# Counting the conv slices and the transfers double, and fetching one step-size tile earlier, in a two-layer kernel (convolutional layer and selective scan)

## The chip, the core and the metric

The kernel runs on one core of one Trainium2 chip. The metric is the device time of one execution in microseconds (us). The core's engines are TensorE (PE, matrix multiply; its weight loads are shown as PEld), VectorE (DVE), ScalarE (ACT), GpSimd (POOL) and SyncE (SP). In this kernel SP issues every DMA. Each engine takes its own instructions strictly in order and waits, where it must, on semaphores.

## What is computed

The input x is 16 images of 64 x 64 pixels with 96 channels in float32. Two layers follow one another, each with a group normalisation in front and a residual sum behind:

```
x = x + L0(gn(x))   # upsample 64->100 by a spectral filter, h = W1 u, h = c0 + c1 h + c2 h^2, W2 h, downsample
x = x + L1(gn(x))   # xz = x Win; xc = silu(conv3x3(xc)); z = silu(z)
                    # 4 directions: delta = softplus(...); h_t = exp(delta_t A) h_(t-1) + delta_t u_t B_t; y_t = C_t h_t
                    # sum of directions, layer norm, times z, times Wout
```

The scan is the large part: 4 directions x 192 channels x 16 states, each over 4096 pixels.

## The kernel before, in words

**The scan, in units.** `scan()` cuts one image into 8 steps (4 pieces of 1024 pixels, first for directions pair 0, then in the opposite order for pair 1), a step into 6 blocks of channels, a block into 4 quarters j = 0 to 3 of the states. One such piece is a *unit* n: 192 units to an image, 3072 in all. A unit has two halves e = 1 and e = 0, each 128 partitions x 1024. Its work is

- ACT: `decay`, da = exp(delta a), once for each half (L788), into PSUM;
- POOL: `drive`, b = dtu * bt for both halves at once (L794), issued two units ahead;
- DVE: `recur`, the scan itself (L803 or L805), once for each half, and the product with ct for half 0 (L972);
- the product with ct for half 1: on POOL (L963), or, in every fifth unit by a running credit (`SHARE`), on DVE (L954). Such a unit is called *odd* below;
- `keep` (L811): the last column goes to the next step's start, for half 1 by DVE (by ACT in an odd unit);
- PE: `read_out` of the unit before (L827), 16 matmuls that sum the states into y.

The order within a unit is written out by hand (L947 to L994): recur(n,1), its product, decay(n+1,1), **slot 0**; POOL's product, drive(n+2); recur(n,0), read_out(n-1), **slot 1**; DVE's product for half 0, decay(n+1,0), **slot 2**; then DMA issues for what comes later.

**What runs in the slots.** Three generators give the other work, a slice at a time (a slice is what stands between two `yield`s):

- `project` makes delta, delta*u and the rows B and C for the next step (PE, ACT, one DVE product at L702, DMAs to DRAM); it has its own pace (`PSLICES`);
- `front(mi+1)`, the first layer of the next image, its norms, and at the end the 3x3 convolution of the second layer with silu: 12 tiles (L482 to L510), 4 with 64 rows (i = 1), 8 with 128 rows (i = 0);
- `finish(mi-1)`, the end of the second layer of the image before; it starts when `front` has ended.

**The pace.** `Background` counts slots in `at` and slices in `n`. A slice is due while n * positions < at * slices. For front and finish positions is 576 (192 units x 3 slots) and slices is `SLICES` = 499. A slice that yields nothing counts 1 and one that yields HEAVY counts 2. A slice that yields WAIT counts 1 too: it ends ahead of the two silu of a convolution tile, and the next slice then runs only in a slot 2 in which it is due (the *gate*, L887); the unit after a gate is made odd (`full_unit`). The credit goes negative by that and no other unit is odd until it is made up, so the number of odd units stays 614.

A silu needs another table in ACT than exp does. A gate therefore puts on ACT: a table load, silu of c_ps (L506), silu of z_ps (L507), a table load back (L508). The two PSUM banks that front and finish share (`b_ps`, bufs=2) hold c_ps and z_ps until then.

**The transfers and tiles that the change touches.** `parts` (L196) moves one image of 96 or 128 rows in 4 (or 2) DMAs, one to a slice: the load of x (L250), the store of x1 (L453), the store of the transposed convolution (L514), the loads of ycol in finish (L529, L530). `fetch_delta` (L726) loads the step sizes of one half of a block (128 x 1024, 512 KB). The pool has three buffers. For the next block, half 1 is fetched in the unit with j = 1, half 0 in the unit with j = 2, behind slot 2 (L980); half 0's buffer is the one that decay(n+1,1) of this same unit reads last.

In `norm` (called twice in front) DVE multiplies two columns of 96 x 1, nb = nmean * rg (L237); behind the first norm it adds 96 x 96, lin = lin + ident (L260).

Of the kernel before, what the change touches and what calls it, by code (L numbers as in the profile page):

```python
# [68 lines left out]
NEPS = 1e-5  # L69
BOTH = "natural_log_exp_and_others"  # L70
POS = 3 * 8 * 6 * NQ
SLICES = 499
WAIT = -1
BUSY = -2
HEAVY = 2
# [5 lines left out]
def tile_two_blocks(  # L81
# [114 lines left out]
    def parts(out, in_, n=4):  # L196

        step = L // n
        for i in range(n):
            nc.sync.dma_start(out=out[:, step * i:step * i + step], in_=in_[:, step * i:step * i + step])  # L200
            yield

    def norm(xt):

# [36 lines left out]
    def front(mi):  # L241
# [225 lines left out]
        for i, n, tiles, both in ((1, 64, 4, 4), (0, 128, 8, 0)):  # L467
            col = b16.tile([128, tiles * TB], F32, name="col", tag="b16")
            halves = [(n * k, t0) for k, t0 in enumerate((0, both)[:128 // n])]
            turned = None  # L470

            def turn(t, row, z):
                nc.scalar.copy(
                    col.rearrange("c (w h) -> c w h", w=HW)[:, :, 8 * t:8 * t + 8],
                    row.rearrange("c (h w) -> c w h", w=HW),
                )
                for p, t0 in halves:
                    cols = slice(TB * (t + t0), TB * (t + t0) + TB)
                    nc.sync.dma_start(out=made["xs"][2 * i, 0:n, cols], in_=row[p:p + n])
                    nc.sync.dma_start(out=made["z"][128 * i:128 * i + n, cols], in_=z[p:p + n])  # L480

            for t in range(tiles):  # L482
                c_ps = bank([128, 8, HW], "c_ps")
                for tap in range(9):
                    dy, dx = divmod(tap, 3)
                    for p, t0 in halves:
                        h0 = 8 * (t + t0) + dy
                        nc.tensor.matmul(  # L488
                            c_ps[p:p + n], lhsT=wtap_s[:, tap, 128 * i:128 * i + n],
                            rhs=xgp[:, h0:h0 + 8, dx:dx + HW], start=(tap == 0), stop=(tap == 8),  # L490
                            skip_group_check=True,
                        )
                    if tap == 3 and turned is not None:
                        turn(*turned)
                    if tap % 2 == 1:
                        yield
                z_ps = bank([128, 8, HW], "z_ps")
                for p, t0 in halves:
                    h0 = 8 * (t + t0) + 1
                    nc.tensor.matmul(  # L500
                        z_ps[p:p + n], lhsT=zwt_s[:, 128 * i:128 * i + n], rhs=xgp[:, h0:h0 + 8, 1:HW + 1],
                        start=True, stop=True, skip_group_check=True,
                    )
                yield WAIT
                row, z = piece([128, TB], "row"), piece([128, TB], "z")
                nc.scalar.activation(row, c_ps.rearrange("c h w -> c (h w)"), AF.Silu, bias=convb_s[:, i:i + 1])  # L506
                nc.scalar.activation(z, z_ps.rearrange("c h w -> c (h w)"), AF.Silu)  # L507
                nc.scalar.preload_act_table_set(BOTH)  # L508
                turned = t, row, z
                yield  # L510
            turn(*turned)
            yield HEAVY
            if i == 0:
                yield from parts(made["xs"][1], col)  # L514
            else:
                for p, t0 in halves:
                    to = made["xs"][2, 64:128, :].rearrange("c (w h) -> c w h", h=HW)
                    for w0 in range(0, HW, 16):
                        nc.sync.dma_start(
                            out=to[:, w0:w0 + 16, 8 * t0:8 * t0 + 32],  # L520
                            in_=col[p:p + n].rearrange("c (w h) -> c w h", w=HW)[:, w0:w0 + 16, :],
                        )
                        yield HEAVY
# [99 lines left out]
    def scan():  # L623


        with ExitStack() as es:
# [99 lines left out]
            def fetch_delta(ctx, bi, e):  # L726
                t = p3.tile([128, T], F32, name="delta")
                spread(t, "delta", ctx, bi, e)
                return t
# [21 lines left out]
            bc, dtus, deltas = {}, {}, {}  # L751
# [103 lines left out]
            class Background:  # L855
# [11 lines left out]
                def step(self):  # L867
                    self.said = next(self.gen, 0)
                    if self.said == 0:
                        self.gen = None  # L870
                    else:
                        self.n += self.said if self.said is not None and self.said > 0 else 1

                def drain(self):
                    while self.gen is not None:
# [40 lines left out]
            for n, (st, bi, j) in enumerate(units):  # L916
                mi, pair, lc = steps[st]
                v, s0, r = blocks[bi]
                m = n // NQ
                if n % per_image == 0:  # L920
                    image[mi]["y"] = dram.tile([2, DI, L], F32, name="y_d")
                    behind_gen.drain()
                    ahead_gen = behind_gen = nothing
                    if mi + 1 < B:
                        ahead_gen = Background(front(mi + 1), SLICES, POS)
                elif n % per_image == 2 and mi > 0:
                    behind_gen = Background(finish(mi - 1), SLICES, POS)
                if j == 0:
                    new = stp.tile([128, 2, NQ], F32, name="new", tag=f"st{bi}")
                    states[bi] = (states[bi][1] if states[bi] else None, new)  # L930

                if j == 0:
                    ahead = None
                    if bi + 1 < len(blocks):
                        ahead = ctxs[st], bi + 1
                    elif n + NQ <= last:
                        step_gen.drain()
                        ahead = ctxs[st + 1], 0
                        next_step(st + 2, mi)
                    if ahead:  # L940
                        dtus[m + 1] = fetch_dtu(*ahead)
                elif j == 1:
                    if ahead:
                        deltas[m + 1, 1] = fetch_delta(*ahead, 1)


                credit += 1  # L947
                odd_here = n == full_unit or credit >= SHARE
                if odd_here:
                    credit -= SHARE  # L950
                h = das[n, 1] if odd_here else bs[n][:, 1, :]
                recur(n, 1, h)
                if odd_here:
                    nc.vector.tensor_mul(bs[n][:, 1, :], h, bc[1, r, j])  # L954
                keep(n, 1, h, nc.scalar.copy if odd_here else nc.vector.tensor_copy)
                if n < last:
                    decay(n + 1, 1)
                slot(0)
                if storing is not None:
                    next(storing, 0)  # L960
                    storing = None
                if not odd_here:
                    nc.gpsimd.tensor_mul(h, h, bc[1, r, j])  # L963
                if n + 2 <= last:
                    drive(n + 2)

                h = das[n, 0]
                recur(n, 0, h)
                if n >= 1:
                    read_out(n - 1)  # L970
                slot(1)
                nc.vector.tensor_mul(bs[n][:, 0, :], h, bc[1, r, j])  # L972
                keep(n, 0, h, nc.scalar.copy)
                if n < last:
                    decay(n + 1, 0)
                if n >= 1 and units[n - 1][2] == NQ - 1:
                    storing = store(n - 1)
                    next(storing)
                slot(2)
                if j == 2 and ahead:  # L980
                    deltas[m + 1, 0] = fetch_delta(*ahead, 0)
                if j == NQ - 1 and n < last and steps[units[n + 1][0]][1] == 1:
                    st2, bi2, _ = units[n + 1]
                    y0s[steps[st2][2], bi2] = fetch_y0(steps[st2][2], bi2)


                at = n % per_step
                for what in range(2):
                    ahead_j = at - (2 * NQ - 1 + what)
                    if 0 <= ahead_j < NQ:  # L990
                        bc[what, 1, ahead_j] = fetch_bc(ctxs[st], 1, ahead_j, what)
                    ahead_j = at - (5 * NQ - 1 + what)
                    if 0 <= ahead_j < NQ and st + 1 < len(steps):
                        bc[what, 0, ahead_j] = fetch_bc(ctxs[st + 1], 0, ahead_j, what)  # L994
# [113 lines left out]
```

## Time and profile before

| what | value |
|---|---|
| median of 3 runs | 21079.41 us (21074.11 to 21098.74) |
| the profiled execution's own time | 21085.42 us |
| its span, first to last instruction | 21083.6 us |
| granted TensorE clock, mean | 0.860 |
| DMA queue of SP, share of 16 engines | 60.1% |

The page gives busy time by engine over the whole span, then groups of instructions. A group's line has its count, its total busy time, the mean of one in ns, and behind the bar the idle time of its engine just before it with what ended most of it. A line of a timeline has the start in us, the duration, engine, line, operation, and in brackets the idle time before it with its releaser.

### The profile page before, as it was taken

The page shows a single profiled execution, that of the slowest core. Times are in us where ns is not written, and L with a number is a line of the kernel's source. Part 1 is how long each engine was busy: PE and PEld are TensorE (multiplying, and loading weights), DVE is VectorE, ACT ScalarE, POOL GpSimd, SP SyncE. Part 2 cuts the span into 40 slices and gives each one's busy share as a digit, 9 for nine tenths or more (in the row PEclk, how much of TensorE's full clock was granted, in tenths as well). Part 3 has the DMA queues.
Part 4 walks back from the last instruction along what each step waited for, and adds up shares of the span by engine and source line. Part 5 has one row for each costly group of instructions (what it writes and reads, how often), then busy time and mean ns, then how long its engine had stood idle before and what let it go on. Part 6 is the DMA issues. An engine that isn't in the chain of part 4 may idle for free. (4 is left out here: it accounts for less than half of the span.)

```text
span 21083.6 us, 273452 instructions
## 1 busy us (share of the span) xinstructions
PE 16908.7 (80%) x98988; PEld 7230.6 (34%) x98988; DVE 19569.4 (93%) x12983; ACT 13780.9 (65%) x20546; POOL 19498.8 (92%) x5538
## 2 busy tenths in 40 slices
PE   7876788888878788788788888888787787888856
PEld 4423324233343333324333242333433333243221
DVE  0999999999999999999999999999999999999997
ACT  4666666667666666666666666676666666666553
POOL 0999999999999999999999999999999999999996
PEclk8887888888889888898888988888898888988977
DMA  2565565655656566565665656556565665656654
GB/s 84 191 202 195 195 227 195 221 202 196 226 198 227 197 210 212 194 230 191 218 207 197 226 199 219 202 197 222 197 226 198 212 212 198 229 195 216 224 186 141
DMA packets 1855464, 4277.11 MB, mean 203 GB/s; under 512 B 449438, under 2 KB 548670, under 8 KB 1852062
## 3 DMA queue, kind: packets, MB, share of 16 engines
q1 hardware_dynamic: 1854110, 4259.62, 60.1%
q8 instruction: 781, 12.80, 0.3%
q14 instruction: 573, 4.69, 0.1%
HBM read 3380.58 MB, written 878.18 MB: 202 GB/s over the span
## 5 line engine op out<-in xcount | busy, mean ns | idle before, releaser
L794 POOL TENSOR_TENSOR b<-dtu,bt 128x2048 f32<-128x2048 f32 x3072 | 13895.8, 4532 | 581.2 <-DMA dtu<-dtu_d 465.1
L788 ACT ACTIVATE da<-delta,a_s 128x1024 f32<-128x1024 f32 x6144 | 6857.4, 1117 | 2562.1 <-DVE b L972 945.5
L963 POOL TENSOR_TENSOR b<-b,ct 128x1024 f32<-128x1024 f32 x2458 | 5797.1, 2358 | 836.9 <-DVE new L811 628.6
L827 PE MATMUL y<-b,fold_s 128*32 128x256 f32 x49152 | 3871.3, 437 | 1153.0 <-DVE b L972 680.8
L972 DVE TENSOR_TENSOR b<-da,ct 128x1024 f32<-128x1024 f32 x3072 | 3756.4, 1223 | 91.8
L803 DVE TENSOR_TENSOR_SCAN da<-da,new,b 128x1024 f32<-128x1024 f32 x1383 | 3245.3, 2347 | 72.7 <-ACT da L788 57.2
L805 DVE TENSOR_TENSOR_SCAN da<-da,new,b 128x1024 f32<-128x1024 f32 x1361 | 3193.0, 2346 | 99.7 <-ACT da L788 77.0
L827 PEld LDWEIGHTS y<-b,fold_s 128*32 128x32 f32 x49152 | 1388.5, 119 | 3876.9 <-issue 1464.0
L805 DVE TENSOR_TENSOR_SCAN b<-da,new,b 128x1024 f32<-128x1024 f32 x943 | 2208.7, 2342 | 139.3 <-ACT da L788 81.5
L803 DVE TENSOR_TENSOR_SCAN b<-da,new,b 128x1024 f32<-128x1024 f32 x921 | 2156.5, 2341 | 11.2 <-ACT da L788 10.5
L811 ACT COPY new<-da 128x1 f32<-128x1 f32 x2764 | 432.9, 157 | 2607.4 <-DVE b L972 2236.0
L488 PE MATMUL c_ps<-xgp,wtap_s 96*64 96x512 f32 (+1 forms) x4608 | 1728.2, 633 | 184.7 <-ACT row L506 179.4
L697 PE MATMUL s<-w,ident_s 128*128 128x512 f32 x1530 | 1167.2, 854 | 636.0 <-ACT w L692 614.2
L371 PE MATMUL h_ps<-xu,w1t_s 96*128 96x500 f32 x1920 | 1044.0, 643 | 299.9 <-ACT t L311 125.9
L383 PE MATMUL o_ps<-w2c_s,hsq 128*100 128x96 f32 x9600 | 1041.5, 266 | 178.1 <-ACT hsq L352 177.8
L677 PE MATMUL s<-pr,dtw_s 128*128 128x512 f32 x1530 | 928.5, 691 | 315.2 <-ACT delta L703 224.9
L805 DVE TENSOR_TENSOR_SCAN da<-da,b 128x1024 f32<-128x1024 f32 x482 | 1103.5, 2289 | 53.0 <-ACT da L788 43.1
L383 PEld LDWEIGHTS o_ps<-w2c_s,hsq 128*100 128x100 f32 x9600 | 975.0, 179 | 410.3 <-ACT hsq L352 232.1
L803 DVE TENSOR_TENSOR_SCAN da<-da,b 128x1024 f32<-128x1024 f32 x460 | 1053.0, 2289 | 36.8 <-ACT da L788 34.8
L697 PE MATMUL s<-e,ident_s 128*128 128x512 f32 x1530 | 1004.2, 745 | 0.0
L820 PE MATMUL y<-y,ident_s 128*128 128x512 f32 x768 | 524.2, 770 | 583.5 <-ACT yt L838 457.6
L488 PEld LDWEIGHTS c_ps<-xgp,wtap_s 96*64 96x64 f32 (+1 forms) x4608 | 583.1, 169 | 1121.7 <-issue 842.6
(143 smaller groups left out, 21936.5 us busy)
## 6 DMA issues: line engine op xcount, KB each, us to landing
dtu<-dtu_d SPq DMA_DIRECT2D x1536, 512.0 KB
delta<-delta_d SPq DMA_DIRECT2D x1536, 512.0 KB
bt<-rows SPq DMA_DIRECT2D x1024, 512.0 KB
ct<-rows SPq DMA_DIRECT2D x1024, 512.0 KB
u<-xs_d SPq DMA_DIRECT2D x893, 256.0 KB
dtu_d<-dtu SPq DMA_DIRECT2D x765, 256.0 KB
delta_d<-delta SPq DMA_DIRECT2D x765, 256.0 KB
xr<-in_x SPq DMA_DIRECT2D x768, 128.0 KB
```

The lines of the kernel that those rows point to most:

```text
L371: nc.tensor.matmul(h_ps[j], lhsT=w1t_s[:, 128 * j:128 * (j + 1)], rhs=xu.rearrange("c p q -> c (p q)"), start=True, stop=True,)
L383: nc.tensor.matmul(o_ps[:, p, :], lhsT=hsq[j][:, UPS * p:UPS * (p + 1)], rhs=w2c_s[:, j, :], start=(j == 0), stop=(j == HB - 1),)
L488: nc.tensor.matmul(c_ps[p:p + n], lhsT=wtap_s[:, tap, 128 * i:128 * i + n], rhs=xgp[:, h0:h0 + 8, dx:dx + HW], start=(tap == 0), stop=(tap ...
L677: nc.tensor.matmul(s, lhsT=dtw_s[:, pair, v, :], rhs=pr, start=True, stop=True)
L697: nc.tensor.matmul(s, lhsT=ident_s, rhs=of, start=(k == 0), stop=(k == 3))
L788: nc.scalar.activation(da, deltas[n // NQ, e], AF.Exp, scale=a_s[:, k, g, units[n][2]:units[n][2] + 1])
L794: nc.gpsimd.tensor_mul(b, dtus[n // NQ], bt.unsqueeze(1).to_broadcast([128, 2, T]))
L803: nc.vector.tensor_tensor_scan(out, da, b, before, ALU.mult, ALU.add)
L805: nc.vector.tensor_tensor_scan(out[:, ::-1], da[:, ::-1], b[:, ::-1], before, ALU.mult, ALU.add)
L827: nc.tensor.matmul(y[32 * q:32 * q + 32, e, :], lhsT=fold_s, rhs=b[:, e, QT * q:QT * q + QT], start=(pair == 0 and j == 0 and e == 0), sto ...
L963: nc.gpsimd.tensor_mul(h, h, bc[1, r, j])
L972: nc.vector.tensor_mul(bs[n][:, 0, :], h, bc[1, r, j])
```

## The change

```
-SLICES = 499
+SLICES = 541
...
     def parts(out, in_, n=4):
...
             nc.sync.dma_start(out=out[:, step * i:step * i + step], in_=in_[:, step * i:step * i + step])
-            yield
+            yield HEAVY
...
                 nc.scalar.activation(z, z_ps.rearrange("c h w -> c (h w)"), AF.Silu)
                 nc.scalar.preload_act_table_set(BOTH)
                 turned = t, row, z
-                yield
+                yield HEAVY
...
                 def step(self):
...
-                        self.n += self.said if self.said is not None and self.said > 0 else 1
+                        self.n += self.said if self.said is not None and self.said > 0 else HEAVY if self.said == WAIT else 1
...
                 slot(0)
+                if j == 2 and ahead:
+                    deltas[m + 1, 0] = fetch_delta(*ahead, 0)
...
                 slot(2)
-                if j == 2 and ahead:
-                    deltas[m + 1, 0] = fetch_delta(*ahead, 0)
```

No instruction is added or taken away. Every slice of `parts`, and two of the six slices of each convolution tile (the one that ends in WAIT and the one with the silu), count 2 instead of 1; the pace of front and finish is 541 counts to 576 slots instead of 499; and the fetch of delta for half 0 is issued behind slot 0 of its unit instead of behind slot 2.

More of the change, by code (lines that the diff above doesn't have):

```diff
@@ L71 @@
 POS = 3 * 8 * 6 * NQ
-SLICES = 499
+SLICES = 541
 WAIT = -1
@@ L200, in parts @@
             nc.sync.dma_start(out=out[:, step * i:step * i + step], in_=in_[:, step * i:step * i + step])
-            yield
+            yield HEAVY
     def norm(xt):
@@ L509, in front @@
                 turned = t, row, z
-                yield
+                yield HEAVY
             turn(*turned)
@@ L871, in step @@
                     else:
-                        self.n += self.said if self.said is not None and self.said > 0 else 1
+                        self.n += self.said if self.said is not None and self.said > 0 else HEAVY if self.said == WAIT else 1
                 def drain(self):
@@ L958, in scan @@
                 slot(0)
+                if j == 2 and ahead:
+                    deltas[m + 1, 0] = fetch_delta(*ahead, 0)
                 if storing is not None:
@@ L979, in scan @@
                 slot(2)
-                if j == 2 and ahead:
-                    deltas[m + 1, 0] = fetch_delta(*ahead, 0)
                 if j == NQ - 1 and n < last and steps[units[n + 1][0]][1] == 1:
```

## The prediction

> **What bounds the kernel now.** I read the page first: two engines are nearly full, and no chain shows one culprit (its largest share is 1%).
>
> ```profile
> ## 1 busy us (share of the span) xinstructions
> PE 16908.7 (80%) x98988; PEld 7230.6 (34%) x98988; DVE 19569.4 (93%) x12983; ACT 13780.9 (65%) x20546; POOL 19498.8 (92%) x5538
> ```
>
> Then POOL's groups. POOL does nothing but two products, and their number is fixed, so its time is a floor; what can be gained is its idle time.
>
> ```profile
> L794 POOL TENSOR_TENSOR b<-dtu,bt 128x2048 f32<-128x2048 f32 x3072 | 13895.8, 4532 | 581.2 <-DMA dtu<-dtu_d 465.1
> L963 POOL TENSOR_TENSOR b<-b,ct 128x1024 f32<-128x1024 f32 x2458 | 5797.1, 2358 | 836.9 <-DVE new L811 628.6
> ```
>
> The 465.1 us are the start-up (image 0's front, alone). The rest I placed from the trace's rows: idle ahead of each POOL product, by unit, and the time from one image's first scan to the next. The 15 images that have a front behind them take 1279.7 us on average (1272.6 to 1287.7); the last, without one, 1225. A unit's POOL work is 4.53 + 0.8 x 2.36 = 6.42 us, so 192 units are 1232 us, and POOL idles 60.6 us an image (908.8 / 15). Of these, about 31.5 us fall in units 106 to 146, the convolution (units 104 to 140); 8.5 us in units 5 to 19 (first norm), 8.3 us in units 99 to 105 (second norm), 8.0 us in units 20 to 98, 4.0 us behind. The last image has 16.6 us in all. So: **two engines in balance, POOL a little ahead as the floor, and half of the loss in a fifth of the image.**
>
> The stretch of the convolution, by windows of image 5 (columns: us; then busy us and count of PE, PEld, DVE, ACT, POOL; clock; DMA share; GB/s): four tiles, a transfer, eight tiles, a transfer, and the five units of the second line below.
>
> ```profile
> 7700.00:7835.00 135.00, 125.05 (x541) 48.93 (x539) 124.27 (x83) 102.57 (x141) 117.14 (x33) 0.96 0.55 187
> 7741.00:7779.00 38.00, 37.99 (x167) 15.44 (x166) 32.62 (x22) 29.99 (x42) 27.75 (x9) 0.98 0.67 224
> ```
>
> In the second line PE is busy for all of 38 us and POOL for 27.75: here neither DVE nor POOL but PE is late. The timeline of the gate inside it:
>
> ```profile
> 7749.52 1.28 ACT L506 ACT_TABLE_LOAD   x1
> 7753.63 0.69 ACT L506 ACTIVATE row<-c_ps,convb_s 128x512 f32<-128x512 f32 x1 [2.83 <-PE c_ps L488]
> 7754.49 0.60 ACT L507 ACTIVATE z<-z_ps 128x512 f32<-128x512 f32 x1 [0.17 <-PE z_ps L500]
> 7755.10 1.28 ACT L508 ACT_TABLE_LOAD   x1
> ...
> 7757.81 2.35 DVE L805 TENSOR_TENSOR_SCAN b<-da,new,b 128x1024 f32<-128x1024 f32 x1 [2.09 <-ACT da L788]
> ...
> 7760.49 2.35 POOL L963 TENSOR_TENSOR b<-b,ct 128x1024 f32<-128x1024 f32 x1 [3.31 <-DVE new L811]
> ```
>
> ACT loads the table, waits 2.83 us for c_ps, and the exp behind it comes late; DVE waits 2.09 us for that exp, POOL 3.31 us for DVE. A gate's own ACT work is 1.28 + 0.69 + 0.60 + 1.28 = 3.85 us.
>
> **The change, part by part.**
>
> *Pace and conv counts (SLICES 541, WAIT and silu slices 2).* Front counted 368 and ends at 368 x 576 / 499 = slot 425 (unit 141). Now it counts 368 + 12 (parts) + 24 (12 tiles x 2) = 404 and ends at 404 x 576 / 541 = slot 430 (unit 143). A tile takes 6 x 576 / 499 = 6.93 slots = 2.31 units now and 8 x 576 / 541 = 8.52 slots = 2.84 units then; all else of front comes 541/499 = 8.4% denser, and the convolution starts at unit 99 instead of 104. Counting slices through gives the gates. Before: 106, 109, 111, 113; 122, 125, 127, 129, 131, 134, 137, 139. After: 101, 105, 107, 110; 119, 122, 125, 127, 130, 133, 137, 139. So gates two units behind another fall from six (111, 113, 127, 129, 131, 139) to three (107, 127, 139).
>
> POOL's idle between a gate and the next, mean of images 1 to 14: for those six 6.10, 2.99, 6.33, 3.26, 4.14, 1.96, mean 4.13 us. For the other six (106, 109, 122, 125, 134, 137) 0.82, 0.88, 0.34, 1.83, 1.32, 1.48, mean 1.11 us. Sum 31.45. After: 3 x 4.13 + 9 x 1.11 = 22.4; giving gates at distance three or four their own mean (1.38) and the first of a run 0.58, 23.2. I take 23.2: **8.2 us an image less.** Ends: if the three cost like the cheapest pair (1.96 and 2.99, mean 2.5), 17.5 and 14 less; like the dearest (6.2), 28.4 and 3 less. The reason that the mean should hold: ACT's waits for c_ps (L506) come only at 111 (1.14), 127 (3.90), 129 (1.53) and 131 (1.74 us), all two behind another and with a single slot from the z_ps matmul to the silu. Afterwards only three tiles have a single slot, the others three to seven. PE's load in the eight tiles falls too: 125 of 135 us before; 8 x 0.53 = 4.2 more units bring 27 us of time (6.4 each), of which the stalls gone take 8, but only some 11 us of PE work (a unit: 1.07 for the 16 matmuls of L827, an estimated 1.6 for project): 136 of 154, 88%. When the stall goes, DVE is late next: an odd unit costs it about 1.1 us more, and gates at three make one unit in three odd. That part stays.
>
> *Denser front, units 8 to 95.* Nothing new is issued; the same work lies 8.4% closer. ACT is 67% busy there (379 of 562 us), PE 82% (462.8). POOL's 8.0 us of idle in units 20 to 98 grow by 8% if they go with density, 0.7; I take +1 us; ends 0 and +5.
>
> *First norm.* nb (L237) moves from unit 6 slot 2 to unit 7 slot 2, lin (L260) from unit 7 slot 2 to unit 8 slot 1. These DVE products of two SBUF tiles stand still while POOL runs:
>
> ```profile
> 7557.02 4.49 POOL L794 TENSOR_TENSOR b<-dtu,bt 128x2048 f32<-128x2048 f32 x1
> 7561.48 2.35 POOL L963 TENSOR_TENSOR b<-b,ct 128x1024 f32<-128x1024 f32 x1
> 7563.80 4.48 POOL L794 TENSOR_TENSOR b<-dtu,bt 128x2048 f32<-128x2048 f32 x1
> 7574.53 2.35 POOL L963 TENSOR_TENSOR b<-b,ct 128x1024 f32<-128x1024 f32 x1 [6.25 <-DVE new L811]
> ```
>
> nb began at 7560.16 and took 8.14 us, to 7568.30: to the end of the last of three POOL products. Behind slot 2 one scan (2.35) stands between the release and POOL's next L963; behind slot 1, a product more (1.22). So lin costs +1.2, taken as **+1 us an image**; ends -1 and +5 (the worst images of the second norm idle 13.2 where the mean is 8.3). The second norm's nb moves from unit 101 slot 0 to unit 96 slot 0, five units, the odd units' own period: 0. The Trainium skill, SBUF — State Buffer, "SBUF: two separate sides", says that a VectorE operation with two SBUF inputs and a GpSimd operation exclude each other and that the loser waits for the one that started first to end; by that rule nb would cost at most one product. The row differs: it lasted over two starts of POOL, and up to 12.3 us in other images, so here the wait ends when POOL pauses. By the rule the ends of this term would be -1 and +1.
>
> *Delta earlier and parts spread.* ACT's waits for delta are 123.9 us in 56 times, at two units of an image above all (144 and 148, 4 to 5 us each), behind the burst of four 512 KB stores and six loads of ycol.
>
> ```profile
> ACT da L788 <- DMA delta<-delta_d: 123.9, 56, 5.3
> ```
>
> Both parts of the change shorten that, but POOL idles only 1.4 us in units 144 to 151, where no unit is odd and POOL's 6.88 us a unit hide DVE. So -1 us; ends -2 and 0. What is moved: the fetch waits on SP for decay(n+1,1), issued on ACT just ahead of slot 0; behind it on SP now stand what slots 1 and 2 issue (project's and front's DMAs). Those were made by instructions later on ACT and DVE anyway; only loads (xr, u) lose a few us of a lead of several slots: 0. finish starts at slot 430 and ends at unit 190 as before: 0.
>
> Sum: -8.2 + 1 + 1 - 1 = -7.2 us an image, x 15 = **-108 us**; 21085.4 - 108 = 20977. The median shown is 6 us below the profiled execution, so 20970.
>
> **The rivals.**
> 1. *Spacing is not what costs* (same). If each of the 12 gates costs its 2.6 us (31.45 / 12) wherever it stands, conv gives 0 and the rest +1 an image: 21,094; anything from 21,040 to 21,100. For it: gate 139 stands two behind another and cost 1.96, gate 125 three behind and 1.83. Against: 6.1 and 6.3 at 111 and 127.
> 2. *PE gets colder* (slower). The clock was 0.96 to 1.00 in the crowded conv windows and 0.85 in the front stretch (units 8 to 95); c_ps matmuls took from 590 to 1222 ns. If spreading lets the clock fall to 0.85, PE's 88% becomes 101% (0.98 x 0.88 / 0.85) and the eight gates of the 128-row tiles cost 4.13 each, the other four 1.11: 37.5 us, +6.0 an image, with +1 from the rest +105 us: 21,185. It decides from a clock of about 0.91 down, where PE's load passes 95%. Against: PE's gaps there are short.
> 3. *All gates get cheap* (faster). At 1.1 to 1.4 us each: 13 to 17 us, 14 to 18 less an image: 20,830 to 20,870.
>
> **How the numbers follow.** Forecast 0.62 (20,880 to 21,035), rival 1 0.17, rival 2 0.12, rival 3 0.09. A measurement tells some 0.2% (42 us) from no change, so faster is below 21,037: 0.62 + 0.09 = 0.71; same 0.17; slower 0.12. The range runs from 20,860 to 21,100, which leaves out rival 2 and half of rival 3.
>
> **What would show it.** POOL's idle before L963 by DVE new falls from 628.6 to some 500 us; ACT's wait for c_ps (170.3 us, 72 times) falls below 100; ACT's wait for delta falls below 60 us; PE is no longer full in any window of 38 us; the clock there stays above 0.93. Wrong if POOL's idle in the conv stretch stays at 31 us an image, if nb and lin take longer than 10 us on average, or if the gain sits in units 8 to 95.

## The result, and the profile after

The changed kernel takes 21084.27 us (median of 12 runs) against 21084.57 us for the kernel before (12 runs); the ratio is 0.9999, 95% interval 0.9991 to 1.0007. That is no difference that can be told. Predicted were 20970 us and a gain of 0.5%.

The page of the changed kernel: span and busy times, then POOL's two groups (L965 is the product that stood in L963).

```profile
span 21080.5 us, 273502 instructions
## 1 busy us (share of the span) xinstructions
PE 16801.4 (80%) x98988; PEld 7116.5 (34%) x98988; DVE 19514.0 (93%) x12983; ACT 13777.9 (65%) x20546; POOL 19499.7 (93%) x5538
...
L794 POOL TENSOR_TENSOR b<-dtu,bt 128x2048 f32<-128x2048 f32 x3072 | 13902.2, 4534 | 522.6 <-DMA dtu<-dtu_d 465.0
...
L965 POOL TENSOR_TENSOR b<-b,ct 128x1024 f32<-128x1024 f32 x2458 | 5805.7, 2362 | 892.1 <-DVE new L811 453.4
```

POOL's work is the same, and so is its idle time: 581.2 + 836.9 before, 522.6 + 892.1 after. The waits of POOL in the changed kernel show where a reader can be misled:

```profile
POOL b L965 <- DVE new L811: 453.4, 249, 16.7
POOL b L965 <- issue: 310.2, 79, 13.8
```

The wait for DVE's `new` fell as forecast (628.6 to 453.4), but the part put down to "issue" rose from 131.1 to 310.2 us. Both come from a late DVE: in 78 of the 79 waits put down to "issue" a `new` of DVE had ended less than 0.3 us before the product began. So only their sum counts, and it stayed: 760 and 764 us.

Placed by unit as in the prediction (us of POOL idle an image, mean of images 1 to 14; the second norm stands in units 99 to 105 before and 94 to 100 after):

| stretch | before | predicted | after |
|---|---|---|---|
| units 0 to 19 (first norm) | 8.5 | 9.5 | 4.9 |
| up to the second norm | 8.0 | 9.0 | 7.2 |
| second norm | 8.3 | 8.3 | 8.5 |
| convolution, to unit 146 | 31.5 | 23.3 | **34.9** |
| rest | 4.0 | 3.0 | 3.6 |
| sum | 60.4 | 53.2 | 59.1 |

14 images gain 1.3 us each, image 0 loses 14.9 us (63.6 to 78.5), the last is even: -3.3 us, and the spans differ by -3.1. So the question is why the convolution did not get cheaper. Its windows in image 5 (the conv from unit 120 on; the five units around gate 127):

```profile
7700.00:7850.00 150.00, 128.95 (x550) 50.50 (x550) 136.26 (x90) 111.95 (x154) 130.00 (x37) 0.91 0.54 181
7751.50:7789.00 37.50, 33.67 (x155) 13.27 (x154) 33.21 (x22) 28.45 (x40) 30.39 (x9) 0.96 0.75 251
```

PE did come down, from 38.0 of 38 us to 33.7 of 37.5, and POOL is fuller there. That step held. The loss went elsewhere, to gates that were cheap before. POOL's idle behind each gate:

| before: gate | 106 | 109 | 111 | 113 | 122 | 125 | 127 | 129 | 131 | 134 | 137 | 139 |
|---|---|---|---|---|---|---|---|---|---|---|---|---|
| us | 0.8 | 0.9 | 6.1 | 3.0 | 0.3 | 1.8 | 6.3 | 3.3 | 4.1 | 1.3 | 1.5 | 2.0 |
| **after: gate** | 101 | 105 | 107 | 110 | 119 | 122 | 125 | 127 | 130 | 133 | 137 | 139 |
| us | 6.6 | 0.6 | 5.5 | 1.3 | 0.0 | 3.6 | 1.8 | 5.2 | 3.3 | 3.8 | 1.5 | 1.7 |

The timeline of gate 101 in the changed kernel, image 5:

```profile
7576.90 0.60 ACT L685 ACTIVATE e<-s 128x512 f32<-128x512 f32 x1 [3.00 <-PE s L677]
7577.53 0.63 ACT L686 ACTIVATE e<-e 128x512 f32<-128x512 f32 x1
...
7579.38 1.28 ACT L506 ACT_TABLE_LOAD   x1
...
7581.87 1.28 ACT L508 ACT_TABLE_LOAD   x1
...
7584.57 2.29 DVE L805 TENSOR_TENSOR_SCAN b<-da,b 128x1024 f32<-128x1024 f32 x1 [1.62 <-ACT da L788]
...
7587.19 2.37 POOL L965 TENSOR_TENSOR b<-b,ct 128x1024 f32<-128x1024 f32 x1 [3.37 <-issue]
...
7588.35 0.71 ACT L692 ACTIVATE w<-w,one_s 128x512 f32<-128x512 f32 x1
...
7589.51 1.12 PE L697 MATMUL s<-w,ident_s 128*128 128x512 f32 x2
...
7593.25 0.69 DVE L702 TENSOR_TENSOR dtu<-s,u 128x512 f32<-128x512 f32 x1 [1.86 <-PE s L697]
...
7596.47 2.36 POOL L965 TENSOR_TENSOR b<-b,ct 128x1024 f32<-128x1024 f32 x1 [2.43 <-DVE new L811]
```

`project` works on ACT in a chain: abs and exp (L685, L686), relu and w (L688, L689), ln and w (L691, L692); then come four matmuls on PE (L697) and one product on DVE (L702). Here the chain has begun when the gate opens. ACT first waits 3.00 us for project's matmul, which stands on PE behind convolution taps, then runs the gate's 3.85 us, and only then the rest of the chain; a first stall of DVE (1.62) follows. The chain's last step ends twelve us after its first began. PE, at the next taps until then, starts the four matmuls of L697 0.45 us after that, and DVE, which has its product L702 in order between two scans, stands for 1.86 us. POOL idles twice, 3.37 and 2.43 us. Below, a gate is called *straddled* when its silu are issued between e and ln of one chain. In the kernel before three of twelve are straddled (109, 122, 125), in the changed one five (101, 122, 125, 130, 133).

### The profile page after: what moved, and what is told of

Read it like the earlier page. It is cut to its first block, busy times and chain, and to the rows that moved or that the text cites. A ratio compares the mean times of both kernels' runs of the same rounds, so it can differ in the third digit from the quotient of the medians.

```text
span 21080.5 us, 273502 instructions
## 1 busy us (share of the span) xinstructions
PE 16801.4 (80%) x98988; PEld 7116.5 (34%) x98988; DVE 19514.0 (93%) x12983; ACT 13777.9 (65%) x20546; POOL 19499.7 (93%) x5538
## 3 DMA queue, kind: packets, MB, share of 16 engines
q1 hardware_dynamic: 1854110, 4259.62, 60.6%
## 5 line engine op out<-in xcount | busy, mean ns | idle before, releaser
L794 POOL TENSOR_TENSOR b<-dtu,bt 128x2048 f32<-128x2048 f32 x3072 | 13902.2, 4534 | 522.6 <-DMA dtu<-dtu_d 465.0
L965 POOL TENSOR_TENSOR b<-b,ct 128x1024 f32<-128x1024 f32 x2458 | 5805.7, 2362 | 892.1 <-DVE new L811 453.4
L488 PE MATMUL c_ps<-xgp,wtap_s 96*64 96x512 f32 (+1 forms) x4608 | 1784.0, 652 | 299.1 <-ACT row L506 293.7
L697 PE MATMUL s<-w,ident_s 128*128 128x512 f32 x1530 | 1185.5, 867 | 685.4 <-ACT w L692 640.3
L383 PE MATMUL o_ps<-w2c_s,hsq 128*100 128x96 f32 x9600 | 993.7, 260 | 99.1 <-ACT hsq L352 66.4
L697 PE MATMUL s<-e,ident_s 128*128 128x512 f32 x1530 | 1032.6, 765 | 0.0
L383 PEld LDWEIGHTS o_ps<-w2c_s,hsq 128*100 128x100 f32 x9600 | 928.3, 172 | 298.2 <-issue 128.1
```

The costliest lines, as they stand in the source:

```text
L383: nc.tensor.matmul(o_ps[:, p, :], lhsT=hsq[j][:, UPS * p:UPS * (p + 1)], rhs=w2c_s[:, j, :], start=(j == 0), stop=(j == HB - 1),)
L488: nc.tensor.matmul(c_ps[p:p + n], lhsT=wtap_s[:, tap, 128 * i:128 * i + n], rhs=xgp[:, h0:h0 + 8, dx:dx + HW], start=(tap == 0), stop=(tap ...
L697: nc.tensor.matmul(s, lhsT=ident_s, rhs=of, start=(k == 0), stop=(k == 3))
L794: nc.gpsimd.tensor_mul(b, dtus[n // NQ], bt.unsqueeze(1).to_broadcast([128, 2, T]))
```

## The experiments

Theory A (the spacing theory of the expectations) is that of the prediction: a gate two units behind another is dear. Theory B (the alignment theory): a gate is dear where it straddles project's chain or where PE is late, and the change only moved the gates to other places of the chain. "After" is the changed kernel. A ratio is to the kernel before as measured beside the run; differences to after are between medians taken at different times, over which the kernel before moved from 21084.6 to 21095.3 us.

**One part at a time, e1 to e3.** e1 is the kernel before with the delta fetch moved alone:

```
                 slot(0)
+                if j == 2 and ahead:
+                    deltas[m + 1, 0] = fetch_delta(*ahead, 0)
...
                 slot(2)
-                if j == 2 and ahead:
-                    deltas[m + 1, 0] = fetch_delta(*ahead, 0)
```

> The kernel before with one part of the change: delta of half 0 is fetched behind slot 0 instead of behind slot 2. The gates stand as before. Spacing theory (mine, as predicted: a gate two units behind another costs 4.1 us of POOL idle, another 1.1) and alignment theory (a gate is dear where the softplus chain of project, from its first exp to w, straddles it or where PE is late with c_ps, wherever the gates stand) both say: POOL idle between units 106 and 146 stays at 31.5 us an image, time within 0.1% (0 to -25 us). If the early fetch holds up SP, slower by more than 40 us.

Measured: ratio to before 0.9998 (0.9989 to 1.0007), 31.9 us in the convolution. ACT's waits for delta fell from 123.9 to 75.1 us, and nobody gained by it.

e2 counts the slices of `parts` double:

```
-SLICES = 499
+SLICES = 515
...
-            yield
+            yield HEAVY
```

> The kernel before with the slices of parts counted double, and 515 slices so that front ends in the same slot (380 x 576 / 515 = 425). Gates 106, 109, 111, 113, 121, 125, 127, 129, 131, 133, 135, 137: eight of twelve stand two behind another; two are straddled by the chain. Spacing theory: conv idle 8 x 4.1 + 4 x 1.1 = 37 us an image, 80 us slower than before. Alignment theory: about as before (two straddled instead of three, more tiles of one slot), 28 to 34 us, same time within 40 us.

Measured: 1.0000 (0.9991 to 1.0009); 32.1 us in the convolution, though eight gates stand two behind another; A said 37. Waits for delta: 76.4 us. With both parts, in the changed kernel, they are 1.2 us, still without effect on the time.

e3 counts double the slice behind the silu and, in `step`, the one that ends in WAIT:

```
-SLICES = 499
+SLICES = 531
...
-                yield
+                yield HEAVY
...
-                        self.n += self.said if self.said is not None and self.said > 0 else 1
+                        self.n += self.said if self.said is not None and self.said > 0 else HEAVY if self.said == WAIT else 1
```

> The kernel before with two slices of each conv tile counted double, and 531 slices so that front ends in the same slot (392 x 576 / 531 = 425). Gates 101, 103, 106, 109, 118, 121, 125, 127, 130, 133, 135, 138: three of twelve two behind another (103, 127, 135), but five straddled by the chain (101, 106, 109, 125, 130, 133 counting the one whose chain had just begun: six). Spacing theory: conv idle 22 to 23 us an image, some 125 us faster than before. Alignment theory: 35 us or more, no faster than before.

Measured: **1.0148 (1.0134 to 1.0162), slower by 313 us**; 44.2 us in the convolution. The straddled gates 106, 109, 130, 133 cost 6.3, 6.3, 5.2, 2.9; the straddled 101 and 125 only 0.8 and 0.9. The rest of the loss lies behind the convolution (10.8 instead of 4.0 us) and ahead of it (12.2 instead of 8.0). A falls as the whole story: it had said 125 us faster.

**The gates moved by a unit or two, e4.**

```
+        for _ in range(2):
+            yield
         for i, n, tiles, both in ((1, 64, 4, 4), (0, 128, 8, 0)):
```

> The changed kernel with two empty slices ahead of the convolution, so that the gates move by one or two units: 102, 105, 107, 110, 119, 122, 125, 129, 131, 134, 137, 139. As in the changed kernel three stand two behind another; but only two (122, 125) are straddled by the chain of project, where five are in the changed kernel (101, 122, 125, 130, 133). Spacing theory: as the changed kernel, within 25 us. Alignment theory: three straddled gates fewer at some 3 us each, 9 us an image, 100 to 150 us faster than the changed kernel.

Measured: 21017 us, ratio to before 0.9964 (0.9951 to 0.9976), 67 us faster than after. The convolution fell from 34.9 to 26.2 us, in sum as B said (9 us). Gate by gate it is less clear: 102, 129 and 134 cost 1.2, 0.9 and 1.5 (101, 127 and 133 had cost 6.6, 5.2 and 3.8), but 125, straddled as before, rose from 1.8 to 5.8, and 131, now two behind another, cost 5.5. Moreover behind the convolution 4.3 us came back (3.6 to 7.9), so that the time gained less than forecast.

**What makes a gate dear, e6, e10 and e12.** e6 and e10 put `AF.Identity` for `AF.Silu` in L506 and L507; e6 drops the table request of L508, e10 keeps it for the first tile of an image.

> The changed kernel with Identity in place of both silu of the convolution and no table loads; what is left out is the silu and the two loads. The gates stand as in the changed kernel; a gate's ACT block falls from 3.85 to 1.3 us, PE's work is the same. Alignment theory with ACT as the cause (the block holds up the chain of project and the exps): POOL idle in units 101 to 146 falls from 34.9 us to some 15, about 300 us faster than the changed kernel. If PE's taps are the cause (c_ps and the matmuls of project late): it stays above 28 us, less than 110 us faster. Spacing theory says nothing on the difference between the gates, but expects the order of them to stay.

e6 took 1.0322 times the time of before (1.0307 to 1.0338) and tells nothing of the gates: without the request, exp (L787 there) and ln (L690) loaded their tables in turn, all over the image.

```profile
L690 ACT ACT_TABLE_LOAD x765 | 981.5, 1283 | 13.3
L787 ACT ACT_TABLE_LOAD x748 | 959.7, 1283 | 13.1
```

> The changed kernel with Identity in place of both silu of the convolution, and the table asked for once an image only, so that exp and ln stay in one table; left out are the silu and their table loads. A gate's ACT block falls from 3.85 to 1.3 us, gates and PE work stay. If ACT's block is what holds the chain and the exps up: conv idle from 34.9 to 13 to 18 us, 250 to 330 us faster than the changed kernel. If PE's taps are: above 28 us, less than 110 us faster. (The run without any request for the table made exp and ln load their tables in turn and told nothing of this.)

e10: 20822 us, 0.9871 (0.9858 to 0.9885), 262 us faster than after; 17.7 us in the convolution, with 122 at 0.4, 130 at 0.9 and 133 at 1.3.

e12:

```
-                    for p, t0 in halves:
+                    for p, t0 in halves if tap in (0, 2, 4, 6, 8) else ():
```

> The changed kernel with five of the nine taps of the convolution; four taps' matmuls are left out. PE's work for a tile falls by four ninths (9.0 to 5.0 us), gates and ACT's block stay. If PE's lateness (c_ps, and project's matmuls behind the taps) is what makes the gates dear: conv idle falls from 34.9 to 15 to 20 us, 220 to 300 us faster than the changed kernel, and the gates 107 and 127 become as cheap as 139. If ACT's block alone is: above 28 us, less than 110 us faster.

e12: 20881 us, 0.9901 (0.9887 to 0.9915), 203 us faster than after; 23.1 us in the convolution, 122 at 0.8, 133 at 2.1; 107 and 127 fell only to 4.3 and 3.9. e10 is what was forecast for ACT's block as the cause; e12 lies between its two forecasts. So neither is it alone: of the 23 us that twelve gates cost over the cheap 1.0 each, ACT's block carries 17.2 and PE's taps 11.9, which is more than the whole together. That fits two parts of one chain, each of which lengthens it.

**The gate kept off the chain, e7 and e9.** One condition more at L887:

```
-                gate = back.said == WAIT and back.due() and position == 2 and storing is None
+                gate = back.said == WAIT and back.due() and position == 2 and storing is None and step_gen.said != BUSY
```

> The changed kernel, in which a gate also waits until project's next slice is not one of its busy ones. Gates 102, 106, 110, 113, 119, 123, 126, 130, 134, 137, 139, 141: none is straddled by the chain (five were), two stand two behind another (three did). Alignment theory: conv idle falls from 34.9 us to 18 to 22, 190 to 250 us faster than the changed kernel. Spacing alone would give one dear gate fewer, 3 us an image, 45 us.

e7: 20849 us, 0.9888 (0.9873 to 0.9903), 235 us faster than after; 17.2 us in the convolution, as B said.

> The kernel before (conv slices and parts counted once) with the gate that waits until project's next slice is not a busy one, and 505 slices so that finish still ends within its image. Gates 106, 110, 113, 115, 121, 123, 126, 130, 134, 137, 139, 141: none straddled, four two behind another (six before). Alignment theory: conv idle falls from 31.5 us to 17 to 22 as it did on the changed kernel (17.2), 150 to 220 us faster than before: the double counting is not needed for it. Spacing theory: four dear gates instead of six, 6 us an image, 90 us.

e9, the same condition on the kernel before, with 505 for `SLICES` in place of 499: 20843 us, 0.9885 (0.9872 to 0.9899), some 250 us faster than before. Here the convolution (from unit 106 on) kept 26.1 us, since 123 and 141, both two behind another and with one slot, cost 5.8 and 6.6; the mid stretch and the second norm gained too (8.0 to 2.0, 8.3 to 5.2), which B had not said. The time is as forecast, its place only in part. The double counting is not needed for the gain.

**The chain moved, the gates kept, e13 and e14.** All runs so far that moved the straddling moved gates. These two change the empty slices at the start of `project` (four before) and its pace; shown is e13, e14 has 73 and 6 in their place:

```
-PSLICES = 71
+PSLICES = 68
...
-                for _ in range(4):
+                for _ in range(1):
                     yield
```

> The changed kernel with project's chain moved instead of the gates: one empty slice at the start of project instead of four, 68 slices to its pace. All twelve gates stand in the units and slots of the changed kernel; only one (105) is straddled by the chain, where five were (101, 122, 125, 130, 133: 19.1 us of POOL idle together). If the straddling makes them dear: those five fall to some 1.0 each, conv idle from 34.9 to 20 to 24 us, 150 to 220 us faster than the changed kernel. If it is where the gates stand, or that they moved at all: as the changed kernel within 40 us.

e13: 20989 us, 0.9948 (0.9935 to 0.9962), 95 us faster than after. The convolution fell from 34.9 to 19.8 us with every gate in its place: 101 from 6.6 to 0.9, 122 from 3.6 to 0.6, 125 from 1.8 to 0.9, 130 from 3.3 to 1.5, 133 from 3.8 to 2.2; 107 (two behind another) stayed at 5.7. 127, two behind another and not straddled in either kernel, fell too, from 5.2 to 2.4, and its wait for c_ps from 2.8 us to none. So the chain's place counts for such a gate as well. The time gained less than 150, because 4.8 us came back ahead of the second norm and 4.9 behind the convolution. Gate 101 again, image 5:

```profile
7545.00 0.71 ACT L692 ACTIVATE w<-w,one_s 128x512 f32<-128x512 f32 x1
...
7546.92 1.28 ACT L506 ACT_TABLE_LOAD   x1
...
7549.41 1.28 ACT L508 ACT_TABLE_LOAD   x1
...
7552.12 2.29 DVE L805 TENSOR_TENSOR_SCAN b<-da,b 128x1024 f32<-128x1024 f32 x1
...
7554.52 0.69 DVE L702 TENSOR_TENSOR dtu<-s,u 128x512 f32<-128x512 f32 x1
7554.73 2.36 POOL L965 TENSOR_TENSOR b<-b,ct 128x1024 f32<-128x1024 f32 x1 [0.50 <-POOL b L794]
```

The chain's last step is done ahead of the table load; behind it neither the scan nor L702 waits, and POOL idles 0.50 us instead of 3.37 and 2.43.

> The changed kernel with six empty slices at the start of project instead of four, 73 slices to its pace. The gates stand as in the changed kernel; four are straddled (119, 122, 130, 133), and 101 and 125 no longer. If straddling makes them dear: 101 falls from 6.6 to about 1, 119 rises from 0 to 2 or more, 122, 130 and 133 stay at 3 to 4; conv idle 28 to 33 us, 30 to 100 us faster than the changed kernel.

e14: 21193 us, 1.0049 (1.0036 to 1.0062), slower than after by some 109 us, not faster: a miss in size and sign. 101 did fall (6.6 to 1.3), but 122 and 133, straddled right behind e, rose to 6.0 and 7.5, 119 only to 0.8; 125, no longer straddled, stayed at 1.7; 36.7 us in the convolution, and 3.2 more at the first norm. Which gates are dear moved with the chain; how dear, I could not say beforehand.

**The norms off their standstill, e5; and together with a gate edit, e8 and e11.** e5 is after with

```
-        nc.vector.tensor_mul(nb, nmean, rg)
+        nc.scalar.activation(nb, nmean, AF.Identity, scale=rg)
...
-        k_ps = bank([C, 1], "k_ps")
-        nc.tensor.matmul(k_ps, lhsT=mt_s, rhs=nb, start=True, stop=True)
+        k_ps = bank([C, 1 + C], "k_ps")
+        nc.tensor.matmul(k_ps[:, 0:1], lhsT=mt_s, rhs=nb, start=True, stop=True)
+        nc.tensor.matmul(k_ps[:, 1:], lhsT=ident_s[0:C, 0:C], rhs=ident_s[0:C, 0:C], start=True, stop=True)
...
-        nc.vector.tensor_add(lin, lin, ident_s[0:C, 0:C])
+        nc.vector.tensor_add(lin, lin, k_ps[:, 1:])
```

> The changed kernel with the two operations of the norms that stood still beside POOL taken off that path: nb is made on ACT (Identity with scale rg) instead of on DVE, and lin is added to the identity read from PSUM, so that DVE reads one SBUF tile only. Gates as in the changed kernel. POOL's idle at the first norm (4.9 us an image) and the second (8.5) should fall to 1 to 2 each if it is the standstill of DVE that makes it: 9 to 11 us an image, 140 to 160 us faster than the changed kernel (ratio to before 0.993). If the idle comes from the ACT work of the norms instead, within 25 us of the changed kernel.

e5: 20885 us, 0.9906 (0.9891 to 0.9920), 199 us faster than after. Idle at the first norm 4.9 to 1.0, at the second 8.5 to 0.1 us; the other stretches stayed within 1 us.

> The two empty slices ahead of the convolution (67 us faster than the changed kernel) and the norms off the standstill together. If the two gains are in different stretches of the image and POOL stays the floor, they add: 67 + 150 = some 215 us faster than the changed kernel, ratio to before 0.990. If what one gives is taken back by DVE later, the sum is less than 150 us.

e8 (e4 and e5): 20798 us, 0.9863 (0.9847 to 0.9880), 286 us faster than after; the two add (67 + 199 = 266).

> The gate off the chain (235 us faster than the changed kernel) and the norms off the standstill (200 us faster) together. They lie in different stretches, so POOL as the floor lets them add: some 430 us faster than the changed kernel, 20,650 us, ratio to before 0.980; POOL idle an image near 31 us. If one takes the other's gain back, above 20,720 us.

e11 (e7 and e5): **20716 us, 0.9820 (0.9806 to 0.9833)**, the fastest; 368 of the 434 us that the two gave alone. POOL idles 35.7 us an image (59.1 in after), 19.4 of them in the convolution.

**The gates of seven kernels put together** (before, after, e2, e3, e4, e7, e9: same work, mean idle behind a gate):

| gate | count | mean us | from to |
|---|---|---|---|
| not straddled, three or more units behind another | 37 | 1.0 | 0.0 to 2.7 |
| straddled, three or more behind | 18 | 3.0 | 0.3 to 6.6 |
| not straddled, two behind | 28 | 4.2 | 1.6 to 6.6 |

(One more gate is both: 1.8. With e13 and e14 the means are 1.1, 3.0 and 4.1 us over 50, 23 and 34 gates, and straddled gates range from 0.2 to 7.5.) So A was half of it: the price of a gate two units behind another held on the mean (4.13 from the kernel before, 4.2 over seven kernels), if not for each. The cheap price holds only for gates that are not straddled.

The traces show what goes with a dear straddled gate: whether ACT stood waiting for project's matmul at the chain's first step (L685) ahead of the gate. Of the 24 straddled gates of the nine kernels, nine had less than 0.3 us of this wait and cost 1.3 us on the mean (0.3 to 3.6); eight had 1.9 us or more and cost 5.4 (2.3 to 7.5); the seven between cost 2.5 (0.2 to 6.3). The 122 of the kernel before and the 125 of e3 had no such wait, 101 in the changed kernel had 3.0 us. With five taps (e12) its wait fell to 0.6 us and its price from 6.6 to 2.6. So a gate seems to be dear where PE is late for ACT and ACT's block is then added; no run changed this wait alone.

## Why the prediction was wrong, point by point

- **The step that failed** is "3 x 4.13 + 9 x 1.11 = 22.4; giving gates at distance three or four their own mean (1.38) and the first of a run 0.58, 23.2". The first term was right in its sum: 107, 127 and 139 cost 5.5, 5.2 and 1.7, together the 12.4 us forecast. The nine others cost 22.4 us instead of some 11. Five of them are now straddled and cost 19.1 (3.8 each). The 1.11 came from six gates of which three were straddled too, but cheap ones (0.9, 0.3, 1.8), and I took distance to be all that set the price, without asking what else runs in the unit of a gate. e13 shows it: same gates, chain elsewhere, 15.1 us an image less, of which 13.1 at these five.
- **Gates and pace**: all twelve gates stand where the counting put them, and front ends in slot 430. PE's load of 88% was 86% (128.95 of 150 us); ACT's waits for c_ps fell from 170.3 to 142.1 us, not below 100 as forecast, because 107 now waits 3.6 us on average and 127 still 2.8.
- **Denser front**, +1: measured -0.8.
- **First norm**, +1: measured -3.6, wrong in sign. I let lin wait behind slot 1 for a drive to end. It began while POOL was in the shorter product and got in at its end: 0.44 us instead of 3.05. On the mean of images 1 to 14 lin took 0.4 us (2.5 before) and nb 4.0 (4.8), which is most of the 3.6.

The kernel before, image 5:

```profile
6955.06 3.05 DVE L260 TENSOR_TENSOR lin<-lin,ident_s 96x96 f32<-96x96 f32 x1
6958.03 2.27 DVE L803 TENSOR_TENSOR_SCAN b<-da,b 128x1024 f32<-128x1024 f32 x1
```

The changed kernel, image 5:

```profile
6964.97 2.35 POOL L965 TENSOR_TENSOR b<-b,ct 128x1024 f32<-128x1024 f32 x1 [2.55 <-DVE new L811]
...
6966.99 0.44 DVE L260 TENSOR_TENSOR lin<-lin,ident_s 96x96 f32<-96x96 f32 x1
6967.28 9.00 POOL L794 TENSOR_TENSOR b<-dtu,bt 128x2048 f32<-128x2048 f32 x2
```

- **Second norm**, 0: +0.1, right. **Delta and parts**, -1: -0.4; the waits for delta are gone (123.9 to 1.2 us) and were hidden, as said.
- **x 15**: image 0 behaved otherwise (+14.9 us: 8.2 between the two norms, 5.1 in the convolution; why is not known). It took back most of what the other 14 gave.
- **The rivals**: the time is that of rival 1, but its reason is not right either: the gates do not cost 2.6 us wherever they stand, they range from 0 to 6.6 (to 7.5 in e14). Rival 2 came in part. Its clock did: the granted clock in units 120 to 142, mean of images 1 to 14, fell from 0.93 to 0.89 (0.91 and 0.96 in the two windows above, where I had wanted more than 0.93), and c_ps matmuls took 652 ns on average (633 before). Its load did not: PE was busy for 85% of these units (89% before), not 95%. In e13 the clock was 0.94 again, so a part of what e13 gave back may be the clock's. In e12, with fewer matmuls, it was 0.84 and the gates cost less than in the changed kernel, so a low clock alone does not make them dear. What the clock alone costs was not tried.
- **Small slips** that decide nothing: 3 x 6.2 + 9 x 1.11 is 28.6, not 28.4; and the 1232 us of POOL work an image counts rows that overlap by some 0.03 us each. Its busy time is 19498.8 / 16 = 1218.7 us, which with 60.6 us of idle gives the 1279.7.

## What to carry to other kernels

When two streams of side work are laid into one hand-made order, a slice's price can belong to a pair, the slice and what the other stream is doing then; here a mean taken over the slices of one stream broke when its pace was changed. Look at the slice in the timeline and ask which chain is cut in two by it; a condition that keeps the two apart (e7, one term in an if) gave 1.1% where even spacing gave nothing. And look for small operations that stand still (nb: 96 numbers, up to 12.3 us): moving them to an engine that has room gave 0.9%.

## What the runs showed of the hardware

- DVE's product nb of two SBUF tiles (96 x 1) lasted 0.16 us with POOL at rest and 2.4 to 12.3 us beside POOL, over up to three starts of POOL's products; each time it ended with a product behind which POOL idled 2.5 us or more. The sum lin (96 x 96) beside it always ended with the POOL product in progress (0.4 to 4.3 us; 0.24 with POOL at rest), even where POOL's next product followed at once. The Trainium skill, SBUF — State Buffer, "SBUF: two separate sides", has the second behaviour (whichever starts first has the shared ports for its whole instruction, and the other waits); for nb the measurement differs. What tells the two apart was not tried. With nb on ACT and lin's other operand in PSUM (e5) the standstill is gone.
- A load of ACT's table took 1.28 us. The 1513 of them that exp and ln made in e6 (765 + 748) took 1941 us of ACT, in a kernel 680 us slower than after; e6 had 1821 loads in all, after 389 and e10 21.
